# Four graph layers on one core: block transposes of neighbouring tokens, and a read-back from scratch in four DMAs

## The chip, the cores and the metric

The kernel runs on one core of a Trainium2 chip. A core has five engines that run side by side and wait for each other through semaphores: TensorE (PE, matmuls; PEld is its weight load), VectorE (DVE), ScalarE (ACT), GpSimd (POOL) and SyncE (SP), whose queue issues the DMAs here. The metric is the device time of one execution in microseconds (us), lower is better; for one version it is the median of several executions.

## The reference

The input x is 32 graphs of 512 nodes with 128 features, all float32, and one 512x512 matrix adj of zeros and ones. Four layers follow, each of the form x = x + layer(relu(layernorm(x))):

- Layer 0: features through Wi and an ELU, edge scores sigmoid(target + source) times a mask made of adj, a product of the scores with the features, and two more linear maps.
- Layer 1: five steps of a gated unit. This is the layer that the change touches:

```python
def step(h, _):
    m_in = jnp.einsum('nm,bmd->bnd', in_matrix, h)
    m_out = jnp.einsum('nm,bmd->bnd', out_matrix, h)
    av = jnp.concatenate([m_in, m_out], axis=-1)
    u3 = h @ u3_w.T + u3_b
    z = jax.nn.sigmoid(av @ w3_w.T + w3_b + u3)
    r = jax.nn.sigmoid(av @ w4_w.T + w4_b + u3)
    hv = jnp.tanh(av @ w5_w.T + w5_b + (r * h @ u5_w.T + u5_b))
    h = (1.0 - z) * h + z * hv
    return (h, None)
```

  Both matrices are adj, so the kernel adds the two halves of w3, w4 and w5 together and multiplies by adj once.
- Layer 2: h times a weight, then adj times that, plus a bias.
- Layer 3: a sum over powers 0 to 3 of adj, each with a weight of its own.

## The kernel before

**Layout.** One graph's h has two forms. In the token form a partition is a token within a chunk of 128 (four chunks), and the free axis holds chunk and feature; in the transposed form a partition is a feature and the free axis holds the 512 tokens. The product with adj (`times_adj`, L690 to L701) needs the token form as the stationary operand; everything else in a step of layer 1 works on the transposed form. So after each step h has to be turned back into the token form.

**The turn.** `turned` (L333 to L345) does that without TensorE. A DVE transpose works on blocks of 32x32: L337 cuts the 512 tokens into 16 blocks of 32 and transposes each; the result `blocks` has its tokens of a block on 32 partitions, for each of four groups b of 32 features. Then one DMA writes `blocks` to a scratch buffer m in device memory (L340), and another reads it back (L342) so that the 128 tokens of a chunk lie on the 128 partitions. In block (q, c) before the change are the tokens c\*128 + i\*4 + q for i from 0 to 31: every fourth token. Because of that step the partition of a token is i\*4 + q, and the whole read-back is a single access pattern over 128 partitions with runs of 128 elements (512 bytes). The readers see the result by chunk through `by_chunk` (L347). With 32 graphs and five steps there are 160 turns.

**Who reads the turned h.** After steps 1 to 4, `parts` (L675 to L688): ACT rounds it to the fp32r type (L682, `hi`) and DVE computes the rest (L685, `lo`); the two parts are multiplied with adj in one pass each (L696). After step 5, DVE adds it to x (L374). Before a turn, DVE computes the new h in three operations (L731, L733, L735). Other operations of a step: the products u3, w4, w3, w5, u5 (L357), copies from PSUM on ACT (L352), adds of the gates on DVE (L714), tanhs on ACT (L362), the reset gate's product on DVE (L721).

**What else uses SP.** Loads of a graph's x (L290), stores of results (L796), and in layer 0 a pair per graph (from the fifth graph on): a gather that writes a column of scores into a row of scratch, d (L498), and a spread of that row to all partitions (L512). Layer 0's masked scores are made on DVE (L520) and multiplied on PE (L535); its last products are L562. Layer 3's products are L770 and L779.

**The order.** Every operation is listed with an engine, an assumed duration, a due time and the values that it reads and writes (`op`, L53). `Plan.order` (L98 to L177) then simulates the engines with these assumed times: an engine takes, among the operations whose inputs are known, the one with the earliest due time, if its buffers are free. An operation's results are known at its start plus its duration plus `result`. What comes out is a fixed order of instructions for each engine's queue, which the engines then work off in order. The plan assumes 0.61 us (T_VEC) for the transpose, 1.0 + 4.0 for the write to scratch and 1.0 + 6.0 for the read-back. Several graphs are under way at once; each begins 56 us after the one before in the steady part (PACE), and the steps of layer 1 are due 44.8 us apart. Two arms are written, one for an adj that fp32r holds exactly and one for others; the exact one runs here.

Of the kernel before, what the change touches and what calls it, by code (L numbers as in the profile page):

```python
# [16 lines left out]
P = 128  # L17
# [21 lines left out]
class Plan:  # L39
# [13 lines left out]
    def op(self, eng, us, due, emit, reads=(), writes=(), two=False, keep=0, result=None):  # L53

        o = Op(eng, us, self.RESULT[eng] if result is None else result, emit, two, keep)
        for v in reads:
            o.before.add(v.writer)  # L60
        for v in writes:
            o.before.update(v.readers)
            if v.writer:
                o.before.add(v.writer)
            elif v.kind and v.slot is None:
                o.takes.append(v)
        for v in reads:
            v.readers.append(o)
        for v in writes:
            v.writer, v.readers = o, []  # L70
        o.vals = [v.whole or v for v in dict.fromkeys([*reads, *writes])]
        for v in o.vals:
            v.left += 1
        for v in [*reads, *writes, *o.vals]:
            self.vals[v] = True
        o.before -= {o, None}
        o.due = max([due, *(b.due for b in o.before)])
        for b in o.before:
            b.after.append(o)
        self.ops.append(o)  # L80
# [100 lines left out]
def tile_four_graph_layers(  # L181
# [27 lines left out]
    nc = tc.nc  # L209
    B, N, D = x.shape  # L210
    NC = N // P
# [13 lines left out]
    op = plan.op  # L225
# [19 lines left out]
    def at(v):  # L245
        if v.tile is not None:
            return v.tile
        return places[v.kind][v.slot] if v.whole is None else at(v.whole)[:, v.part]
# [84 lines left out]
    def turned(src, due):  # L333


        blocks, moved, t = Val("f"), Val("m"), Val("f")
        op("DVE", T_VEC, due, lambda: nc.vector.transpose(  # L337
            at(blocks).rearrange("p (q c f) -> p q c f", c=NC, f=32),
            at(src).rearrange("p (c i q) -> p q c i", c=NC, q=4)), [src], [blocks])
        op("SP", 1.0, due, lambda: nc.sync.dma_start(at(moved), at(blocks)),  # L340
           [blocks], [moved], result=4.0)
        op("SP", 1.0, due, lambda: nc.sync.dma_start(  # L342
            at(t).rearrange("p (b e) -> p b e", e=P),
            at(moved).rearrange("(b i) (q e) -> (i q) b e", i=32, e=P)), [moved], [t], result=6.0)
        return t  # L345

    def by_chunk(t):  # L347
# [251 lines left out]
    def list_rest(exact, pool):  # L599
# [104 lines left out]
        def layer1(b, h, due, pace):  # L704
            tok = parts(h, due, two=True)
            h = copied(transposed(h, due), due)
            for t in range(STEPS):
# [29 lines left out]
                h = c  # L737
                d += 5
                h_tok = turned(h, d)
                if t + 1 < STEPS:  # L740
                    tok = parts(h_tok, d + 9, True, by_chunk)
# [120 lines left out]
```

## Time and profile before

| What | Before |
|---|---|
| median of 3 executions | 1757.03 us (1756.03 to 1757.21) |
| profiled execution | 1756.07 us, span of the trace 1754.2 us |
| PE busy | 1697.3 us, 97% of the span |
| PEld busy | 1095.1 us, 62% |
| DVE busy | 1549.1 us, 88% |
| ACT busy | 1049.3 us, 60% |
| POOL busy | 426.4 us, 24% |
| granted TensorE clock, mean | 0.995 |
| DMA issues: m<-f (L340) and f<-m (L342) | 160 each of 256 KB, 2.0 and 2.8 us to landing (median) |
| DMA issues: d<-s (L498) and f<-d (L512) | 28 each, 9.3 and 4.2 us to landing (median) |

How to read the profile: f, r, x, m, d and b are kinds of buffers (f working tiles in SBUF, r the fp32r parts, x the inputs, m and d scratch in device memory, b banks of PSUM), so "m<-f" is the write to scratch and "f<-m" the read-back. "L337" is line 337. A group's line gives the count of instructions, their busy time, the mean of one in ns, and the time that the engine stood idle just before them with what ended it. Busy intervals of consecutive instructions of one engine can overlap, since each is shown from its first read to its last write. SPq and ACTq are the instruction queues of SP and ACT. A DMA's entry on SPq is the time that its issue took there; the transfer itself runs on and is given as the time to landing.

### The profile page before, as it was taken

How to read it: one execution, taken by the hardware profiler on the slowest of the kernel's cores; microseconds unless marked ns; L12 is line 12 of the kernel's file. 1: busy time of each engine (PE TensorE's matmuls, PEld its weight loads, DVE VectorE, ACT ScalarE, POOL GpSimd, SP SyncE). 2: the span in 40 equal slices, each digit the busy share in tenths (PEclk: the TensorE clock that was granted, in tenths of full speed). 3: DMA queues.
4: the chain of work that ended last, by engine and by line, in shares of the span. 5: the costliest groups of instructions: out<-in, count | busy, mean ns of one | idle time of the engine just before them, and what ended most of it. 6: DMA issues, size and time to landing. Idle time of an engine off the chain costs nothing.

```text
span 1754.2 us, 20927 instructions
## 1 busy us (share of the span) xinstructions
PE 1697.3 (97%) x6829; PEld 1095.1 (62%) x6829; DVE 1549.1 (88%) x3277; ACT 1049.3 (60%) x1899; POOL 426.4 (24%) x312
## 2 busy tenths in 40 slices
PE   5899999999999999999999999999999999999998
PEld 3555555566666666666666666666665656566797
DVE  6899899999998889988989899899998979889862
ACT  6665665675666565656665566655756645555441
POOL 4522212332422212222122222122232212001120
PEclk9999999999999999999999999999999999999999
DMA  3012322333222321133212222222221131221201
GB/s 109 7 42 68 83 90 67 79 61 78 44 60 60 79 62 59 55 79 66 72 49 67 73 68 66 66 56 83 72 54 50 42 91 49 84 72 49 84 7 54
DMA packets 164535, 112.08 MB, mean 64 GB/s; under 512 B 23232, under 2 KB 139840, under 8 KB 164416
## 3 DMA queue, kind: packets, MB, share of 16 engines
q1 hardware_dynamic: 164416, 110.65, 23.6%
q8 instruction: 55, 0.90, 0.2%
q14 instruction: 64, 0.52, 0.1%
HBM read 60.23 MB, written 50.39 MB: 63 GB/s over the span
## 4 chain that ended last, share of the span: by engine, by line
PE 66%; DVE 20%; DMA 7%; ACT 4%; issue 2%; SPq 0%; DVEq 0%; ACTq 0%
PE b L357 29%; PE b L696 13%; PE b L779 8%; DMA f<-m 6%; PE b L770 5%; DVE f L520 3%; PE b L535 3%; DVE f L714 2%; PE b L562 2%; DVE f L337 2%; DVE r L685 2%; DVE f L735 2%; PE b L329 2%; DVE f L721 1%; DVE f L733 1%
## 5 line engine op out<-in xcount | busy, mean ns | idle before, releaser
L696 PE MATMUL b<-A_r,r 128*128 128x512 f32 x1536 | 424.3, 419 | 3.0 <-DVE r L685 3.0
L352 ACT COPY f<-b 128x512 f32<-128x512 f32 x448 | 257.4, 587 | 228.4 <-PE b L696 130.9
L696 PEld LDWEIGHTS b<-A_r,r 128*128 128x128 f32 x1536 | 285.4, 188 | 105.3 <-issue 35.2
L391 POOL TENSOR_TENSOR s<-s,nhalf 128x4 f32<-128x4 f32 x128 | 159.8, 1249 | 773.9 <-DVE s L389 761.3
L779 PE MATMUL b<-r,A_r 128*128 128x512 f32 x768 | 308.9, 501 | 0.0
L714 DVE TENSOR_TENSOR f<-f,b 128x512 f32<-128x512 f32 x320 | 211.8, 676 | 36.0 <-PE b L357 34.3
L779 PEld LDWEIGHTS b<-r,A_r 128*128 128x128 f32 x768 | 141.1, 189 | 105.9 <-issue 94.9
L526 POOL TENSOR_TENSOR f<-f,f 128x512 f32<-128x512 f32 x96 | 161.5, 1685 | 178.6 <-DVE f L520 127.8
L362 ACT ACTIVATE f<-f,b4w 128x512 f32<-128x512 f32 x160 | 115.7, 723 | 144.9 <-DVE f L714 144.6
L337 DVE STREAM_TRANSPOSE f<-f 128x512 f32<-128x512 f32 x160 | 175.7, 1101 | 0.3
L357 PE MATMUL b<-f,w4T 128*128 128x512 f32 x320 | 164.7, 597 | 10.2 <-ACT f L352 10.2
L357 PE MATMUL b<-f,u5T 128*128 128x512 f32 x320 | 164.5, 598 | 8.0 <-DVE f L721 7.5
L357 PE MATMUL b<-f,u3T 128*128 128x512 f32 x320 | 163.4, 594 | 3.4 <-ACT f L352 3.4
L357 PE MATMUL b<-f,w3T 128*128 128x512 f32 x320 | 162.9, 592 | 0.0
L357 PE MATMUL b<-f,w5T 128*128 128x512 f32 x320 | 162.1, 592 | 0.0
L685 DVE TENSOR_TENSOR r<-f,r 128x512 fp32r<-128x512 f32 x192 | 131.7, 692 | 29.4 <-ACT r L682 28.7
L770 PEld LDWEIGHTS b<-V,f 128*128 128x128 f32 x1024 | 132.0, 191 | 34.8 <-issue 29.0
L362 ACT ACTIVATE f<-f,b3w 128x512 f32<-128x512 f32 x160 | 115.1, 720 | 62.1 <-DVE f L714 61.8
L731 DVE TENSOR_TENSOR f<-f,f 128x512 f32<-128x512 f32 x160 | 123.7, 776 | 31.7 <-ACT f L362 31.1
L682 ACT CAST r<-f 128x512 fp32r<-128x512 f32 x192 | 117.5, 621 | 50.1 <-DMA f<-m 35.4
L362 ACT ACTIVATE f<-b,b5w 128x512 f32<-128x512 f32 x160 | 109.9, 688 | 60.6 <-PE b L357 59.9
L535 PE MATMUL b<-f,f 128*128 128x512 f32 x256 | 129.1, 593 | 4.3 <-issue 3.2
(97 smaller groups left out, 2577.1 us busy)
## 6 DMA issues: line engine op xcount, KB each, us to landing
m<-f SPq DMA_DIRECT2D x160, 256.0 KB, 2.0
f<-m SPq DMA_DIRECT2D x160, 256.0 KB, 2.8
x<-in_x_dram SPq DMA_DIRECT2D x32, 256.0 KB, 4.3
out_dram<-x SPq DMA_DIRECT2D x32, 256.0 KB, 2.4
f<-d SPq DMA_DIRECT2D x28, 256.0 KB, 4.2
f<-in_adj_dram SPq DMA_DIRECT2D x4, 256.0 KB, 4.6
f<-in_L_gnn_weight_dram SPq DMA_DIRECT2D x2, 224.0 KB, 2.6
d<-s SPq DMA_DIRECT2D x28, 2.0 KB, 9.3
```

Of the source, the lines that this page charges most:

```text
L337: op("DVE", T_VEC, due, lambda: nc.vector.transpose(at(blocks).rearrange("p (q c f) -> p q c f", c=NC, f=32), at(src).rearrange("p (c i q) ...
L352: op("ACT", us, due, lambda: nc.scalar.copy(at(t), at(src)), [src], [t])
L357: op("PE", T_MM, due, lambda: nc.tensor.matmul(at(dst), at(w), at(src), start=start, stop=stop), [src, w], [dst])
L362: op("ACT", us, due, lambda: nc.scalar.activation(at(dst), at(src), AF.Tanh, bias=at(bias), scale=scale), [src, bias], [dst])
L391: op("POOL", 1.2, due, lambda: nc.gpsimd.tensor_tensor(stat(SCALE), stat(VAR), at(neg_half), op=ALU.pow), [s, neg_half], [s])
L526: op("POOL", 1.4, d, lambda: nc.gpsimd.tensor_tensor(at(dst), at(a), at(c), op=ALU.add), [a, c], [dst])
L535: op("PE", T_MM, d, lambda jc=jc: nc.tensor.matmul(at(pn), at(msg)[:, ts(jc, P)], at(es[jc]), start=jc == 0, stop=False), [msg, es[jc]], [pn])
L685: op("DVE", T_VEC, due, lambda: nc.vector.tensor_tensor(part(lo), whole(), part(hi).bitcast(F32), op=ALU.subtract), [src, hi], [lo], two=two)
L696: nc.tensor.matmul(at(pa), at(part)[:, ts(jc, P)], at(adjT)[:, jc, :], start=jc == n == 0, stop=jc == NC - 1 and n == PARTS - 1,)
L714: op("DVE", T_VEC, d, lambda: nc.vector.tensor_tensor(at(s), at(u), at(pg), op=ALU.add), [u, pg], [s])
L770: nc.tensor.matmul(at(pz)[:, ts(i, D)], at(hT[i])[:, ts(ic, P)], at(V[k]), start=i == 0, stop=last and i == G - 1,)
L779: nc.tensor.matmul(at(pz), at(adjT)[:, jc, ts(ic, P)], at(part), start=False, stop=jc == NC - 1 and n == PARTS - 1,)
```

## The change

Each block of the transpose now holds 32 neighbouring tokens: block (q, c) has the tokens c\*128 + q\*32 + i. The transpose reads them with step one, where it read every fourth element; the order of what it writes is as before. The write to scratch is unchanged. A token's partition in the token form is now q\*32 + i, so the read-back goes block by block: for each q one DMA that reads from scratch the columns of that q (four runs of 512 bytes for each of 32 partitions, 64 KB) and writes the partitions q\*32 to q\*32 + 31. Four DMAs are issued one after the other on SP as one operation of the plan. The plan assumes 1.6 us on SP for it, where it assumed 1.0, and 5.4 us until the result is known, where it assumed 6.0; the sum is the same. The other arm's code gets the same change.

```diff
         op("DVE", T_VEC, due, lambda: nc.vector.transpose(
             at(blocks).rearrange("p (q c f) -> p q c f", c=NC, f=32),
-            at(src).rearrange("p (c i q) -> p q c i", c=NC, q=4)), [src], [blocks])
+            at(src).rearrange("p (c q i) -> p q c i", c=NC, i=32)), [src], [blocks])
         op("SP", 1.0, due, lambda: nc.sync.dma_start(at(moved), at(blocks)),
            [blocks], [moved], result=4.0)
-        op("SP", 1.0, due, lambda: nc.sync.dma_start(
-            at(t).rearrange("p (b e) -> p b e", e=P),
-            at(moved).rearrange("(b i) (q e) -> (i q) b e", i=32, e=P)), [moved], [t], result=6.0)
+        def carry():
+            for q in range(4):
+                nc.sync.dma_start(
+                    at(t)[ts(q, 32), :].rearrange("p (b e) -> p b e", e=P),
+                    at(moved)[:, ts(q, P)].rearrange("(b i) e -> i b e", i=32),
+                )
+        op("SP", 1.6, due, carry, [moved], [t], result=5.4)
         return t
```

## Prediction

> **What bounds the kernel now.** I start with the stretches, because shares over the whole span mix stages. Here are the busy times of the engines in four stretches; the columns are the stretch, its length, then PE, PEld, DVE, ACT and POOL (busy, instructions), granted clock, DMA share and GB/s.
>
> ```profile
> 0.00:100.00 100.00, 75.30 (x309) 45.57 (x310) 78.33 (x207) 64.64 (x129) 50.58 (x57) 0.97 0.21 56
> 100.00:500.00 400.00, 385.51 (x1390) 229.43 (x1389) 379.27 (x791) 259.31 (x468) 108.22 (x66) 1.00 0.28 70
> 500.00:1650.00 1150.00, 1137.35 (x4525) 732.56 (x4523) 1036.75 (x2142) 693.92 (x1244) 253.81 (x180) 1.00 0.24 65
> 1650.00:1754.20 104.20, 99.11 (x609) 87.48 (x607) 54.71 (x140) 31.40 (x61) 13.78 (x11) 0.99 0.14 41
> ```
>
> The reader is to see two engines near their limit. From 100 to 500 us VectorE (DVE) is busy 379.3 of 400 us (95%) and TensorE (PE) stands idle for 14.5; later PE leads (1137 of 1150) and DVE has 10% to spare. Clock and DMA are no issue.
>
> How much can be won at all? PE's busy time has modelled ends, so I price its work by the pace inside long pieces of the chain of waits: 20 matmuls of L357 in 8.58 us (0.43 each), 16 of L696 in 3.64 and 24 of L779 in 5.47 (0.228), 48 of L770 in 5.36 (0.112). Counts from the groups: 1736 + 256 fp32 matmuls of 512 columns x 0.43 = 857; 2360 one-pass ones x 0.228 = 538; 2469 of 128 columns x 0.112 = 276. Sum 1671 of 1754.2, so 83 us are no work: 25 in the first 100 us, 5 at the end, **53 in between**. Nothing can win more than that without shortening matmuls.
>
> Next, the chain of work that ended last, by engine and by line:
>
> ```profile
> PE 66%; DVE 20%; DMA 7%; ACT 4%; issue 2%; SPq 0%; DVEq 0%; ACTq 0%
> PE b L357 29%; PE b L696 13%; PE b L779 8%; DMA f<-m 6%; PE b L770 5%; DVE f L520 3%; PE b L535 3%; DVE f L714 2%; PE b L562 2%; DVE f L337 2%; DVE r L685 2%; DVE f L735 2%; PE b L329 2%; DVE f L721 1%; DVE f L733 1%
> ```
>
> The transpose (L337) is on it with 2% (2.1% in the fuller answer, 37 us), the read-back (f<-m, L342) with 6%.
>
> **Part 1, the transpose.** The group and, from the timeline of DVE, its neighbours (start, duration):
>
> ```profile
> L337 DVE STREAM_TRANSPOSE f<-f 128x512 f32<-128x512 f32 x160 | 175.7, 1101 | 0.3
> ```
>
> ```profile
> 303.33 0.68 DVE L714 TENSOR_TENSOR f<-f,b 128x512 f32<-128x512 f32 x1
> 303.93 1.11 DVE L337 STREAM_TRANSPOSE f<-f 128x512 f32<-128x512 f32 x1
> 304.98 0.64 DVE L733 SCALAR_TENSOR_TENSOR f<-f,f 128x512 f32<-128x512 f32 x1
> ```
>
> Durations overlap, so occupancy is start to next start: 0.60 us for L714, 1.05 for the transpose (1.01 to 1.08 at five other places; I take 1.04). The instruction stays, with the same 128x512 elements and the same output order; only its input becomes dense. No DVE row here shows a transpose with dense input. Bounds: at best it becomes an ordinary dense 128x512 op, 0.60; at worst nothing changes, 1.04 (a loss is excluded: nothing but the reading step changes, and towards dense). I take 0.64, near the dense rows, which are alike whatever the operation (L714, L733, L735 all start 0.60 apart), plus 32/512 of 0.60 for one block. That frees 0.40 us x 160 = **64 us of DVE** (0 to 70).
>
> The Trainium skill speaks both ways on this row. "VectorE: DVE Perf Modes", section "The three transpose paths", gives 311 ns for a 128x128 bf16 DVE transpose; scaled to 512 columns that is an estimate of 1.24 us, above the 1.10 measured here, and would make part 1 worth nothing. "SBUF — State Buffer", section "Door 1", says that reads in one 16-byte line run at full rate and each new line costs; the step of four fp32 is just such a line, and by it the sum below stands.
>
> What of the 64 us shows in the end? The chain holds 37 / 1.10 = about 34 transposes, counted where DVE's queue order or data made the end wait: 34 x 0.40 = **14 us**. The other 126 lie beside matmuls. A check by stretch: 100 to 500 us has 46 transposes, 18 us freed in a stretch where PE idles 14.5; two thirds of that, about 10, is plausible, and the PE-led rest may give 4. What is late next is PE's own in-order queue.
>
> **Part 2, four read-backs instead of one.** From the answer on the scratch tile m (min/median/max duration in ns; who waited; time to landing):
>
> ```profile
> L340 SPq DMA_DIRECT2D m<-f  x160: 319/332/497, 96.7 to 1657.2; - x160
> L342 SPq DMA_DIRECT2D f<-m  x160: 359/370/1636, 98.8 to 1661.9; - x160
> ...
>   ACT r L682: 35.4, 11
> ...
>   DVE x L374: 0.2, 1
> ```
>
> An issue holds SP's queue for 0.33 (L340) to 0.37 us (L342), so three more cost 3 x 0.33 = 1.0 us per read-back, 160 in all: 160 us on a queue that issues for some 150 and otherwise waits (L340 for the transpose: 847 us; L342 for m: 259). Behind it in that queue stand the next write to scratch, the loads of x (due 40 us ahead), the stores, and the score row's gather and spread (L498, L512); each may leave 1 us later.
>
> Landing: the read-back takes 2.8 us (median) for 256 KB. The last piece starts 1.0 us later but carries a quarter: between 0.8 earlier (the first three pieces land the bulk; a last one at the 2.0 of m<-f would give 1.0 + 2.0 = 3.0, and less if small) and 1.0 + 2.8 = 3.8, so -0.8 to +1.0; I take +0.3, nearest to the 2.0 row. The cover: the plan allows 7.0 us from issue (1.0 + 6.0; afterwards 1.6 + 5.4, the same), the transfer needs 2.8, and only 12 of 160 read-backs were waited for. If the cover went, each late one would cost its own lateness, up to 1.0 us.
>
> The skill speaks against this part: "SBUF — State Buffer", section "Door 1", measures 32 partitions at 189 GB/s against 328 for 128, an estimate of 4 x 0.35 = 1.4 us instead of 0.8 for this data; and "DMA: Bandwidth & Descriptors", "Rules for kernel authors", says not to split a transfer by partitions. That would be +0.6 us of landing, still under the cover.
>
> The 12 that were waited for have one cause. The timeline of SP, then the chain:
>
> ```profile
> 804.14 0.36 SPq L498 DMA_DIRECT2D d<-s  x1
> 804.59 0.45 SPq L342 DMA_DIRECT2D f<-m  x1
> 805.10 0.50 SPq L290 DMA_DIRECT2D x<-in_x_dram  x1
> ```
>
> ```profile
> 804.59 11.83 DMA f<-m
> ```
>
> A read-back issued right behind the gather (d<-s, 9.3 us to landing) lands after 11.8. That is so behind 11 of 28 gathers, and these make the chain's 6%. Four pieces go out while the gather still drains, so I add 0 (at most 9 on the chain x 1.0 = 9).
>
> **Part 3, added waits.** The readers of t (L682 on ACT in 128 cases, L374 on DVE in 32) need four landings instead of one. Extra wait instructions show as 17 ns on ACT and 21 on DVE: 3 x 0.02 x 160 = 10 us, mostly on ACT, which is busy 60%; queued behind are the copies L352 and tanhs L362, which today wait for PE and DVE anyway. I cost it at 0.
>
> **Part 4, the order.** The plan sees SP taken 0.6 us longer per read-back; due times stay. It can therefore write another order on every queue, worth some us either way; I take 0.
>
> **Sum.** Profiled execution: span 1754.2 + 1.9 around it = 1756.07. Less 14: 1742. The median shown, 1757.03, lies 1 us higher, so **1743**.
>
> **Rivals.**
> - *The transpose stays at 1.10.* For it: no dense transpose in the trace. Against: every dense 128x512 op takes 0.60. Then only SP's extra remains, under cover: 1757 (1753 to 1763).
> - *PE takes all that DVE gives.* For it: DVE at 95% for 400 us, and waits of ACT for L714 of 206 us in all. Against: PE is already busy without a gap in 14 of the 35 windows of 50 us. Half of the 53 us: 1757 - 27 = 1730; all: 1704.
> - *Slower: more read-backs behind gathers.* Place: SP's order of L342 and L498, re-made by part 4. Price: the eleven 50-us windows that hold such a pair lose 23 us of PE, 2.1 each (those at 1310 and 1426 end in PE idling 3.4 and 3.3 us). From 7 more pairs (18 of 28) the 14 us are eaten; with 10 more: 1743 + 21 = 1764. For it: pieces occupy SP longer around each gather. Against: the plan knows the gather's 11 us, and can as well lose pairs.
>
> **Chances.** Forecast 0.55; PE takes more 0.15; transpose unchanged 0.13; slower 0.17. The range reaches from 1722 (a little past half of the slack) to 1765. Measurement tells 0.2% (3.5 us) from no change: faster 0.55 x 0.95 + 0.15 + 0.13 x 0.2 = 0.70; same 0.13; slower 0.17.
>
> **What would show it.** Right: L337 near 0.70 us mean, DVE's busy near 1485, PE's idle from 100 to 500 us near 5, SP with 640 read-back issues of 0.33 and L682 waiting for f<-m in about a dozen places. Wrong: L337 at 1.1; or waits of L682 for f<-m spread over scores of places (the cover gone); or pairs behind gathers counted well above 11.

## The result, and the profile after

The changed kernel takes 1757.34 us (1756.21 to 1759.71), the kernel before 1757.12 beside it: ratio 1.0002, 95% interval 0.9985 to 1.0020. No difference, where 14 us less was forecast. The profiled execution took 1757.87 us, its span 1756.0.

In the changed file the read-back is L344, and every line after `turned` has a number that is four higher (L361 is the old L357, L502 the gather, L686 the cast, L700 the product with adj).

The stretches, with the columns as before (PE, PEld, DVE, ACT, POOL):

```profile
0.00:100.00 100.00, 77.27 (x304) 47.30 (x305) 76.62 (x205) 62.99 (x126) 49.94 (x56) 0.91 0.20 55
100.00:500.00 400.00, 386.09 (x1380) 230.56 (x1379) 365.68 (x790) 256.59 (x465) 94.36 (x65) 0.99 0.27 70
500.00:1650.00 1150.00, 1137.90 (x4547) 734.88 (x4546) 1007.43 (x2153) 697.38 (x1249) 252.60 (x181) 1.00 0.24 65
```

VectorE has the room that was forecast: 365.7 busy from 100 to 500 us, where it was 379.3. TensorE did not use it: idle for 13.9 of these 400 us, where it was 14.5. The transpose is as short as was forecast:

```profile
L337 DVE STREAM_TRANSPOSE f<-f 128x512 f32<-128x512 f32 x160 | 111.8, 702 | 0.3
```

702 ns, where it was 1101. So the change did what it says. The chain of work that ended last shows what stands in its place:

```profile
PE 74%; DVE 11%; DMA 8%; ACT 3%; issue 2%; SPq 2%; DVEq 0%; ACTq 0%
PE b L361 33%; PE b L700 15%; PE b L783 9%; DMA f<-m 7%; PE b L774 5%; PE b L539 4%; PE b L566 3%; PE b L329 2%; DVE f L524 2%; PE b L757 1%; PE b L483 1%; DVE f L725 1%; DVE f L718 1%; SPq L344 1%; DVE r L689 1%
```

DVE fell from 20% to 11% and L337 left the list, but the read-back grew from 6% to 7%, and SP's queue is new with 2%. The answer on scratch tile m says who waited:

```profile
L344 SPq DMA_DIRECT2D f<-m x640: 302/426/1947, 99.8 to 1666.3; - x160
L340 SPq DMA_DIRECT2D m<-f x160: 319/338/4215, 97.8 to 1661.3; - x160
...
  ACT r L686: 52.9, 17
```

The waits of ACT for the read-back went from 35.4 us at 11 places to 52.9 at 17. In the timeline of SP, one of the places:

```profile
308.75 0.37 SPq L502 DMA_DIRECT2D d<-s  x1
309.16 2.12 SPq L344 DMA_DIRECT2D f<-m  x4
311.33 5.69 SPq L290 DMA_DIRECT2D x<-in_x_dram  x1
```

The four pieces go out behind the gather in 2.12 us, and the load after them then held SP's queue for 5.69 us, where such an issue takes 0.5. Counted over the whole timeline, 15 gathers have a read-back directly behind them, where it was 11. This is the place that the forecast's last rival named. Three suspects could have eaten the gain, then: the four pieces, the new order with its 15 pairs, or a gain that never existed.

### The profile page after: what moved, and what is told of

Its sections match the earlier page's. It is cut to its first block, busy times and chain, and to the rows that moved or that the text cites. A ratio compares the mean times of both kernels' runs of the same rounds, so it can differ in the third digit from the quotient of the medians.

```text
span 1756.0 us, 22048 instructions
## 1 busy us (share of the span) xinstructions
PE 1701.2 (97%) x6829; PEld 1100.1 (63%) x6829; DVE 1502.2 (86%) x3277; ACT 1049.3 (60%) x1899; POOL 409.6 (23%) x312
## 4 chain that ended last, share of the span: by engine, by line
PE 74%; DVE 11%; DMA 8%; ACT 3%; issue 2%; SPq 2%; DVEq 0%; ACTq 0%
PE b L361 33%; PE b L700 15%; PE b L783 9%; DMA f<-m 7%; PE b L774 5%; PE b L539 4%; PE b L566 3%; PE b L329 2%; DVE f L524 2%; PE b L757 1%; PE b L483 1%; DVE f L725 1%; DVE f L718 1%; SPq L344 1%; DVE r L689 1%
## 5 line engine op out<-in xcount | busy, mean ns | idle before, releaser
L700 PE MATMUL b<-A_r,r 128*128 128x512 f32 x1536 | 426.5, 421 | 3.7 <-DVE r L689 3.7
L700 PEld LDWEIGHTS b<-A_r,r 128*128 128x128 f32 x1536 | 286.8, 189 | 109.1 <-issue 37.1
L783 PE MATMUL b<-r,A_r 128*128 128x512 f32 x768 | 313.0, 506 | 1.0 <-DVE r L689 1.0
L530 POOL TENSOR_TENSOR f<-f,f 128x512 f32<-128x512 f32 x96 | 152.8, 1592 | 199.5 <-DVE f L524 166.6
L689 DVE TENSOR_TENSOR r<-f,r 128x512 fp32r<-128x512 f32 x192 | 136.4, 712 | 45.9 <-ACT r L686 45.2
L361 PE MATMUL b<-f,w4T 128*128 128x512 f32 x320 | 166.1, 601 | 8.5 <-ACT f L356 8.5
L361 PE MATMUL b<-f,u5T 128*128 128x512 f32 x320 | 165.0, 599 | 9.2 <-DVE f L725 9.0
L361 PE MATMUL b<-f,u3T 128*128 128x512 f32 x320 | 163.5, 596 | 2.3 <-ACT f L356 2.3
L361 PE MATMUL b<-f,w3T 128*128 128x512 f32 x320 | 163.6, 594 | 0.0
L361 PE MATMUL b<-f,w5T 128*128 128x512 f32 x320 | 162.1, 592 | 0.0
L686 ACT CAST r<-f 128x512 fp32r<-128x512 f32 x192 | 118.8, 624 | 69.3 <-DMA f<-m 52.9
L735 DVE TENSOR_TENSOR f<-f,f 128x512 f32<-128x512 f32 x160 | 119.2, 746 | 37.1 <-ACT f L366 36.9
L774 PE MATMUL b<-V,f 128*128 128x128 f32 x1024 | 132.9, 275 | 0.0
```

The lines of the kernel that those rows point to most:

```text
L361: op("PE", T_MM, due, lambda: nc.tensor.matmul(at(dst), at(w), at(src), start=start, stop=stop), [src, w], [dst])
L530: op("POOL", 1.4, d, lambda: nc.gpsimd.tensor_tensor(at(dst), at(a), at(c), op=ALU.add), [a, c], [dst])
L689: op("DVE", T_VEC, due, lambda: nc.vector.tensor_tensor(part(lo), whole(), part(hi).bitcast(F32), op=ALU.subtract), [src, hi], [lo], two=two)
L700: nc.tensor.matmul(at(pa), at(part)[:, ts(jc, P)], at(adjT)[:, jc, :], start=jc == n == 0, stop=jc == NC - 1 and n == PARTS - 1,)
L735: op("DVE", T_VEC, d, lambda c=c, h=h: nc.vector.tensor_tensor(at(c), at(c), at(h), op=ALU.subtract), [c, h], [c], two=True)
L774: nc.tensor.matmul(at(pz)[:, ts(i, D)], at(hT[i])[:, ts(ic, P)], at(V[k]), start=i == 0, stop=last and i == G - 1,)
```

## The experiments

Each ratio is against the kernel before on the same chip, with its 95% interval. Before took 1757 to 1775 us from chip to chip, so between chips only ratios are compared, not times.

### One part at a time

**Dense transpose alone** (one read-back, same plan, same order):

```diff
-            at(src).rearrange("p (c i q) -> p q c i", c=NC, q=4)), [src], [blocks])
+            at(src).rearrange("p (c q i) -> p q c i", c=NC, i=32)), [src], [blocks])
```

> The kernel before with the dense transpose alone: one read-back, the plan's numbers and so the order of every queue as before. The tokens of a chunk then come back in another order, so the values are not the reference's; the work is the same. Theory A (the gain is real and the four read-backs or the new order give it back): 1743, between 1738 and 1750. Theory B (time of VectorE is not on the path, the forecast's 14 us never existed): 1757, between 1754 and 1760, with L337 at 0.70 us and VectorE's busy time near 1490 all the same.

Measured: 1746.31 us, ratio 0.9937 (0.9924 to 0.9949): 11 us less. Theory B is out. From its stretches:

```profile
100.00:500.00 400.00, 388.89 (x1400) 233.00 (x1399) 372.35 (x796) 259.29 (x470) 94.72 (x68) 1.00 0.28 70
500.00:1650.00 1150.00, 1140.62 (x4568) 738.78 (x4567) 1002.57 (x2166) 695.97 (x1246) 247.48 (x178) 1.00 0.24 65
```

In the same stretches TensorE gains 3.4 and 3.3 us of busy time and gets 53 more matmuls done than before (1400 + 4568 against 1390 + 4525). The waits for the read-back are as before (35.0 us at 11 places).

**Four read-backs alone** (transpose with step four, plan's numbers as before):

```diff
+        def carry():
+            for q in range(4):
+                nc.sync.dma_start(
+                    at(t)[ts(q, 32), :].rearrange("p (b e) -> p b e", e=P),
+                    at(moved)[:, ts(q, P)].rearrange("(b i) e -> i b e", i=32),
+                )
+        op("SP", 1.0, due, carry, [moved], [t], result=6.0)
```

> The kernel before with the four read-backs alone: transpose with step four, the plan's numbers as before (1.0 and 6.0). The tokens come back in another order here too. Theory A in its form 'the read-backs give it back': 1765 to 1772. In its form 'the new order gives it back' and by theory B: 1755 to 1760.

Measured: ratio 1.0017 (1.0008 to 1.0026), 3 us more. A cost, but a quarter of what would be needed to eat the 11 us.

**The new order alone**:

```diff
-        op("SP", 1.0, due, lambda: nc.sync.dma_start(
+        op("SP", 1.6, due, lambda: nc.sync.dma_start(
             at(t).rearrange("p (b e) -> p b e", e=P),
-            at(moved).rearrange("(b i) (q e) -> (i q) b e", i=32, e=P)), [moved], [t], result=6.0)
+            at(moved).rearrange("(b i) (q e) -> (i q) b e", i=32, e=P)), [moved], [t], result=5.4)
```

> The kernel before with only the plan's numbers of the read-back changed (1.6 and 5.4), so that the queues get the order of the changed kernel, with one read-back and the transpose of step four. Theory A in its form 'the new order gives it back': 1765 to 1772. In its form 'the read-backs give it back' and by theory B: 1755 to 1760.

Measured: ratio 1.0068 (1.0055 to 1.0080), 12 us more, with the same instructions. The chain, and who waited for tile m:

```profile
PE 67%; DVE 18%; DMA 9%; ACT 4%; issue 2%; SPq 0%; DVEq 0%; ACTq 0%
PE b L357 30%; PE b L696 14%; PE b L779 8%; DMA f<-m 8%; PE b L770 5%; PE b L535 3%; DVE f L520 2%; PE b L562 2%; DVE f L714 2%; PE b L329 2%; DVE r L685 2%; DVE f L337 2%; DVE f L721 2%; DVE s L386 1%; PE b L753 1%
```

```profile
  ACT r L682: 52.6, 15
```

The read-back has 8% of the chain instead of 6%, and the waits are those of the changed kernel (52.9), although it has only one DMA per read-back. They come with the order, not with the pieces.

**Both parts in the old order** (the changed kernel with `op("SP", 1.0, ..., result=6.0)`):

> The changed kernel with the plan's numbers of before (1.0 and 6.0): dense transpose and four read-backs in the order of before. Theory A by the read-backs: 1757, as the changed kernel. Theory A by the order: 1743. Theory B: 1755 to 1760.

Measured: ratio 0.9957 (0.9944 to 0.9970), 8 us less. The parts add up: -0.63% and +0.17% make -0.46, measured -0.43. The changed kernel differs from this one by two numbers of the plan, and those take back 0.45%.

### What in the order costs

If it is the read-backs behind gathers, then a kernel without such pairs must be fast in either order. The issue of the order is edited so that a gather with a read-back directly behind it on SP goes out after it; no other queue changes:

```diff
     def issue(operations):
+        queue = [o for o in operations if o.eng == "SP"]
+        for g, r in zip(queue, queue[1:]):
+            if g.emit.__name__ == "gather" and r.emit.__name__ == "carry":
+                operations.remove(g)
+                operations.insert(operations.index(r) + 1, g)
         with tc.manual_schedule():
```

(`carry` is here the one DMA of before, given a name.)

> The kernel before with the plan's numbers 1.6 and 5.4, and where a gather (L498) stands directly ahead of a read-back on SP (15 places), the gather goes out behind it; every other queue keeps its order. Theory P (the new order costs because 15 instead of 11 read-backs drain behind a gather): this and its partner with the numbers of before come within 4 us of each other, and both are faster than their originals, this one by 15 x 2 to 3 = 30 to 45 at most, so 1725 to 1745. Theory O (the order costs by something else, in other queues): it stays 8 to 14 slower than its partner.

> The kernel before with the same exchange in its 11 places. Theory P: 1725 to 1745, 11 x 2.1 = 23 faster than before by the price in the forecast. Theory O: the waits of ACT for f<-m (35 us) go, and the time stays within 5 us of before, because they lay beside other work.

Measured: new order 0.9849 (0.9832 to 0.9866), order of before 0.9821 (0.9805 to 0.9836). The exchange alone, with the slow transpose, is worth 1.8%: more than was expected of it (31 us on this chip, 2.8 for each of 11 places). The distance between the two orders shrinks from 0.68% to 0.28%; theory P holds for the larger part, and 0.28% is left (6 us between the medians, where at most 4 was expected). The order of before with the exchange, its chain, and what is left of the waits:

```profile
PE 74%; DVE 21%; ACT 3%; issue 2%; DMA 0%; SPq 0%; DVEq 0%; ACTq 0%
```

```profile
ACT r L689 <- DMA f<-m: 2.6, 4, 1.0
```

DMA is off the chain, from 7% to 0; the waits fell from 35.4 us to 2.6. DVE is on it with 21%, with the transpose at 1105 ns.

**Where the exchange gains.** In the profile of the kernel before (span 1754.2 us) and in that of its order with the exchange (1733.1 us) TensorE works off the same 6829 matmuls in the same order, so their starts can be compared. With the exchange the matmul that started at 500 us starts 6.5 us earlier, that of 1300 us 10.1, of 1350 us 15.4, of 1400 us 15.9 and of 1450 us 21.2, and so it stays to the end. Two of the 11 pairs, with their gathers at 1309.5 and 1425.5 us, are thus worth 5.3 us each, and the other nine about 1.2 each. Here is the kernel before around the first of the two: from its chain the read-back and 16 matmuls behind it, the same 16 for another graph without such a wait, and the slice from 1320 to 1330 us (columns as above, the granted clock behind POOL):

```profile
1309.97 11.76 DMA f<-m
1325.31 3.12 PE b L562 x16
1268.22 1.78 PE b L562 x16
1320.00:1330.00 10.00, 6.64 (x25) 4.43 (x24) 5.32 (x9) 7.42 (x15) 0.75 (x1) 0.83 0.29 59
```

TensorE idles for 3.4 us, and then the granted clock of the slice is 0.83 and the 16 matmuls take 3.12 us instead of 1.78. The slice from 1440 to 1450 us, behind the other pair, has 0.83 too; with the exchange every slice of 10 us from 40 us on has 1.00. At these two places the wait cost its idle time and slower matmuls behind it. The runs on this chip say the same: the mean granted clock was 0.987 to 0.993 in the eleven of the kernel before and 0.995 to 0.997 in the five with the exchange. The 0.6% between them, on some 1695 us of TensorE's work, is an estimate of 10 of the 31 us, which would leave the 21 that lie between the two profiles (both at a mean clock of 0.995). Why the clock falls there was not tried.

**Two more orders**, to see whether the count of pairs sets what an order costs (the kernel before with 1.2 and 5.8, or 1.8 and 5.2, in the plan):

> The kernel before with the plan's numbers 1.2 and 5.8: nothing but another order, in which 9 read-backs stand directly behind a gather. If pairs behind gathers set what an order costs: 2 x 2 to 3 us faster than before, 0.2 to 0.35%. If an order is a draw from many causes: anywhere within 0.7% on both sides, without regard to the 9.

> The same with 1.8 and 5.2, 13 pairs. If the pairs set it: 2 x 2 to 3 us slower than before, 0.2 to 0.35%. If it is a draw: anywhere within 0.7%.

Measured: with 9 pairs 0.9997 (0.9986 to 1.0007), with 13 pairs 1.0081 (1.0068 to 1.0095). The count is a poor guide: 9 pairs are no better than 11, 13 are as bad as 15. In the order with 9, ACT waited 50.9 us for read-backs, at 15 places. There is another way to be late behind a gather, which its timeline of SP shows:

```profile
663.34 0.36 SPq L498 DMA_DIRECT2D d<-s  x1
666.09 0.33 SPq L340 DMA_DIRECT2D m<-f  x1
675.58 0.36 SPq L342 DMA_DIRECT2D f<-m  x1
```

Here the write to scratch goes out 2.75 us after the gather, and its read-back, which waits for it, can go only 9.5 us later, where 2.1 is usual. The exchange does not touch such places.

The same two orders with the exchange:

> The kernel before in the order of the plan's numbers 1.8 and 5.2, with the gather behind the read-back in its 13 places. If the read-backs behind gathers make the spread between orders: 0.983 to 0.986 of before, close to the two other orders without pairs (0.982 and 0.985). If the order loses by something else: 0.990 or more, 0.8% behind the first of them.

> The same in the order of 1.2 and 5.8, 9 places. If the pairs make the spread: 0.982 to 0.986 too, although only 9 places are exchanged. If each exchange is worth the same and the rest is a draw: 1.79% x 9 / 11 = 1.5%, so 0.985, and no telling; a value above 0.988 speaks for a draw.

Measured: 0.9902 (0.9885 to 0.9918) and 0.9871 (0.9855 to 0.9888). Both are above the values expected if the pairs made all of the spread, and the first lies where an order that loses by something else was expected (0.990 or more); but the kernel before took 1758.9 on this chip and 1767.6 on that of the first two exchanged orders, so only neighbours on one chip compare: 1.8 against 1.2 was 0.84% apart with pairs and is 0.31% without; 1.6 against 1.0 was 0.68% and is 0.28%. Twice, some 60% of the spread goes with the pairs; that share is rough, since each ratio has an interval of 0.1 to 0.2% on either side. What makes the remaining 0.3% between orders stays open. Late read-backs of the other kind do not explain it: with the exchange ACT waited for read-backs for 1.2 us in the order of 1.6 and for none in that of 1.8, no longer than in the faster orders of 1.0 (2.6 us) and 1.2 (3.1 us).

### Versions that keep the gain

**The changed kernel with the exchange, and its twin in the old order:**

> The changed kernel with the gather behind the read-back in its 15 places (behind all four pieces). Theory P: the waits behind gathers are what ate the gain, so this is 1.5% to 2% faster than before, 1725 to 1732 on a chip where before takes 1757; what stays against its partner in the old order is the 0.3% that the order cost in the pair of runs with one read-back. Theory O: at most 0.5% faster, 1748 or more.

> Dense transpose and four read-backs with the plan's numbers of before, gather behind the read-back in 11 places. By adding what was measured (exchange 1.8%, dense 0.6%, four pieces -0.2%): 2.2% faster than before, 1718 where before takes 1757; if the four pieces lose more once the gathers are out of their way: 1.8% or less.

Measured: 0.9765 (0.9752 to 0.9777) and 0.9748 (0.9735 to 0.9760). Without the pairs the changed kernel is 2.4% faster than before; the order costs it 0.17% then, where it cost 0.45%. Both gain more than was expected (1.5 to 2% and 2.2%). The clock may have a part in it here too: on this chip the mean granted clock was 0.985 to 0.990 in the runs of the kernel before, and 0.993 to 0.998 in those of these two.

**Without step four and without four pieces.** The step can be taken where it costs nothing: by the two copies from PSUM that make the transposed form (L706 and L710 of before), so that the free axis holds every fourth token together and a dense transpose with one read-back gives the old token form:

```diff
+    def copied_apart(src, due, us=T_COPY):
+        t = Val("f")
+        op("ACT", us, due, lambda: nc.scalar.copy(
+            at(t).rearrange("p (c q i) -> p c q i", c=NC, q=4),
+            at(src).rearrange("p (c i q) -> p c q i", c=NC, q=4)), [src], [t])
+        return t
...
-            h = copied(transposed(h, due), due)
+            h = copied_apart(transposed(h, due), due)
...
-                m = copied(times_adj(tok, d), d)
+                m = copied_apart(times_adj(tok, d), d)
```

> A form that needs neither the step of four in the transpose nor four read-backs: the two copies from PSUM on ACT that make the transposed form (of the first h and of the product with adj) put every fourth token together, so the dense transpose and one read-back give the token form as it was; order of the queues as before. If the two effects measured so far are all: 1746, as with the dense transpose alone, if the 192 copies (0.59 us each) stay as long with a step of four in what they read; with 0.4 us more each, 77 us more of ACT, which is busy 60%: 1748 to 1755.

> The same with the gathers behind the read-backs in 11 places. If the gains of the dense transpose and of the exchange add up (theory P): 1746 - 23 = 1723, between 1715 and 1735. Theory O: 1741 to 1750.

Measured: 0.9916 (0.9899 to 0.9933), and with the exchange 0.9765 (0.9750 to 0.9781), 1726.95 us. The copies with and without the step, in the second of them:

```profile
L354 ACT COPY f<-b 128x512 f32<-128x512 f32 x256 | 149.7, 588 | 124.6 <-PE b L366 80.4 <-PE b L329 21.4 <-PE b L710 20.0
L359 ACT COPY f<-b 128x512 f32<-128x512 f32 x192 | 112.4, 589 | 131.2 <-PE b L710 125.2 <-PE b L329 4.2 <-DMA f<-d 1.2
```

L359 reads every fourth element and takes 589 ns, L354 reads densely and takes 588. The chain of this version:

```profile
PE 92%; DVE 5%; ACT 2%; issue 1%; DMA 0%; SPq 0%; DVEq 0%; ACTq 0%
```

This is what a kernel bound by TensorE looks like: 92%, where it was 66%. It and the changed kernel in the old order with the exchange beat both kernels of this case; the two ran on different chips, and which is the faster was not tried.

## Why the prediction was wrong

**Part 1 was right**, in the duration and in what shows of it. The transpose takes 0.40 us less, as assumed (1101 to 702 ns; the next instruction now starts 0.63 after it, where 0.64 was taken), and the end gains 11 us where 14 were read off the chain. Counting the transposes on the chain was a good estimate here. The check by stretch was not: it put about 10 of the 14 us between 100 and 500 us, with TensorE's idle time there near 5 us as a sign; with the dense transpose alone TensorE idles there for 11.1 us, where it was 14.5. Of the two rules of the Trainium skill, the one in "SBUF — State Buffer", "Door 1", agrees with the traces here: 1101 ns with a step of 16 bytes, 702 without. The figure in "VectorE: DVE Perf Modes", "The three transpose paths", scaled to 512 columns (1.24 us), does not: the measurement decides.

**Part 2 was a little too low.** Three more issues were to cost 1.0 us of SP per read-back and nothing at the end. From the start of the first piece to the end of the last, the four take 1.75 us (median), where one read-back took 0.37: 1.4 us more, and 3 us (0.17%) at the end. The added waits of part 3, taken at 0, are in these 3 us and were not run alone. (SP's queue was also fuller than "some 150" us: its issues take 182 us in the profile before. Nothing in the sum rests on it.) The cover did hold: with the four pieces in the old order ACT waited for read-backs for 35.5 us, as before, and for 39.7 with the dense transposes. What makes the 3 us stays open. Held issues like those of 5.7 and 8.6 us in the changed kernel are not it: with the four pieces alone, the load behind the gather and the pieces at 312 us was issued in 0.43 us, and no issue after the first 60 us took more than 1.72.

**Part 4 failed.** "It can therefore write another order on every queue, worth some us either way; I take 0." This is the step that failed: the order was put at nothing without a reason, although its price behind gathers stood among the rivals. Measured alone, the order costs 12 us (0.68%), and 0.45% with the dense transposes. The three parts alone sum to -11 + 3 + 12 = +4 us; the pair of changed kernels gives -8 for both parts and +8 for the order, so 0; measured 0.2. That gain and loss cancel so closely is chance.

For the larger part (some 60% of what the order costs) the mechanism was the one of the last rival, more read-backs behind gathers; the rest of the order's cost stays open. The rival's price was off: it took 2.1 us for each pair, and so needed seven more pairs to eat the gain. Four more came, 11 to 15, in an order that costs 12 us. The exchange gives 2.8 for each place as a mean, but a pair has no one price: in the two profiles two pairs were worth 5.3 us each and nine about 1.2, and orders with 9 and with 11 pairs take the same time. The price was read from TensorE's idle time in 50-us windows, which leaves out that the matmuls behind the longest waits ran slower.

**The two other rivals** are out: the transpose did get shorter, and TensorE did not take more than the chain showed, not before the waits behind gathers were gone.

## What to carry to other kernels

A change of a cost in a planner is a change of every queue: run the plan's new numbers alone before crediting or blaming the code that came with them. Where a slow small DMA and a transfer that is waited for share a queue, look at which goes first; here, exchanging them was worth two to three times the 36% cut of a VectorE instruction (1.8% against 0.63% for the dense transpose alone, and 0.84% for the version with the step in the copies, which ran on the same chip as the exchange). When a wait is priced, look at the matmuls behind it too, not only at the idle time. A step that one engine pays for may be free on another that copies the data anyway.

## What the runs showed of the hardware

- A read-back behind the gather of 512 single elements lands 11.0 to 12.1 us after its issue in the kernel before, where the median of all is 2.8. Four pieces of 64 KB are as late: on the chain of the changed kernel their last piece mostly lands 9.8 to 10.5 us after its own issue, where the median of all pieces is 1.9. With the read-back put ahead of the gather, ACT's waits for it all but went (35.4 to 2.6 us), so it is its place in the queue that makes it late.
- An issue can be held for long. Behind a gather and four pieces the next DMA's issue took 5.69 us at 311 us and 8.60 at 971, where it takes 0.4 to 0.5; 4 of the 15 places show more than 4 us, the others at most 0.45, and with one DMA per read-back it is seen too (7.93 us for a load at 435 us, in the run with the new order alone). From the timeline of SP of the changed kernel:

```profile
968.28 0.38 SPq L502 DMA_DIRECT2D d<-s  x1
968.77 2.02 SPq L344 DMA_DIRECT2D f<-m  x4
970.90 8.60 SPq L800 DMA_DIRECT2D out_dram<-x  x1
```

- An issue of a quarter of the data is not cheaper: 0.43 us (median) for 64 KB in 32 partitions, 0.37 for 256 KB in 128.
- A step of four fp32 elements costs VectorE's transpose from SBUF 57% (1101 against 702 ns, 128x512) and ScalarE's copy from PSUM nothing (589 against 588 ns).
- In the kernel before, where TensorE had idled for 3.4 and 3.3 us behind late read-backs, the granted clock was 0.83 in a slice of 10 us, and 16 matmuls took 3.12 and 2.82 us instead of 1.78.
